# One gate of a GRU recurrence multiplied in exact bfloat16 parts, the other two in float32

## The chip, the cores and the metric

The kernel runs on one core of a Trainium2 chip. The metric is the device time of one execution in microseconds; three runs of the kernel before are given, with their median. A profile comes from one further execution with a hardware trace. In it PE is TensorE (matmuls), PEld the weight loads of TensorE, DVE VectorE, ACT ScalarE, POOL GpSimd and SP SyncE; "q" behind an engine stands for the queue on which it issues DMAs.

## The reference

A GRU runs over time. x has the shape (8, 256, 512), that is 8 rows of 256 time steps of 512 features, and the state has 8 x 512 values.

```
gi = x @ W_ih + b_ih            # 512 -> 3*512
gh = h @ W_hh + b_hh
r = sigmoid(i_r + h_r);  z = sigmoid(i_z + h_z)
n = tanh(i_n + r * h_n)
h = (1 - z) * n + z * h         # one step; 256 of them, each on the one before
```

The 2048 states then pass through a mixture of experts: a router chooses 2 of 8 experts (each 512 to 2x256 and back) by softmax and top 2, and a shared expert (512 to 2x1024 and back) takes all of them. The sum is added to x. Everything is float32.

## The kernel before

The step, which is `step(n)`. The state is kept transposed, `hT` with 128 partitions by 4 quarters `q` by 8 batch rows, in four buffers that take turns (`states`). For each gate in the order r, n, z (the order of `banks`), 16 matmuls are issued: for each quarter q of the 512 inputs, four of them (j), each with the 8 columns of hT as the stationary operand and 128 columns of w_hh as the moving one, and each writing one strip of 32 partitions of the gate's PSUM bank, rows 32j to 32j+8. In the trace each of these float32 matmuls appears as two records. Behind each gate DVE turns the bank with a 32x32 block transpose (`turned`, L489): the gate then lies with the features over the partitions. ACT takes the sigmoid of r (L493), DVE multiplies n's part by r (L496) and adds the part of x (L498), ACT takes the tanh (L500), DVE turns z, ACT takes its sigmoid (L502), and three DVE operations form the new state: `hn = h - n` (L505), `z*hn` (L507), `n + z*hn` (L508). ACT copies the new state into `hc` for the later stages (L511).

The part of x and the biases are put into a gate's bank before its matmuls accumulate onto it: `open_gate` (L458, on ACT) copies them there from `seeds` (r and z) or `seeds_n` (n). In the n bank the rows 32j to 32j+8 hold the bias of the state's product and the rows 32j+8 to 32j+16 the part of x, since r must multiply the first and not the second. `load_seeds` loads the seeds of four steps at a time from DRAM on SP's queue.

x's part is computed ahead, in blocks of 16 steps. `project(k, g)` multiplies the turned x of block k with W_ih for gate g in four pieces, and its end copies the result to `gi` on ACT (L416), adds the bias on POOL (L417) and stores it to DRAM on SP. `transpose_x(k)` (L313, on DVE) turns the block's x and issues the loads of the next one; `turn_x_afterwards` puts it into a list of things to do on DVE "afterwards".

The order of the work is written by a planner in the kernel, without times from the chip. A `queue` holds pieces of matmul work (projections, then the shared expert of finished blocks), and behind each step as many pieces are issued as keep the block even: they are the filler of TensorE while the other engines finish the step. `catch_up(room)` issues DVE work from the list `afterwards` behind each step, up to `WINDOW = 1.1` us by the planner's own costs; a piece that needs something from the list forces it. Routing (`choose`, `sum_logits`, `order_experts`, `weigh`, `count_places`, `give_places`, `send_rows`) is given fixed steps of the block. Weight loads of the experts are put into `loads` and issued one at a time on POOL's DMA queue (L170).

The tile `we` has room for the weights of 8 experts. W_ih lies in the room of experts 6 and 7 and w_hh in that of experts 4 and 5 (`wih`, `whh`) until they are no longer needed: experts 0 to 3 are loaded from block 2 on, 6 and 7 in the last block, 4 and 5 behind the loop. After the loop come the rest of the shared expert, the layout of the lists, and 35 tiles of 128 rows, each through one expert's weights (`gu_t` L722, `yp` L853).

Before the loop, block 0 is projected, x's blocks 0 and 1 are turned on TensorE, one and a half projections of block 1 are made, the list is emptied (`catch_up(None)`), the seeds of the first chunks are loaded, and the three gates of step 0 are opened. POOL's copy of one column of `hn` into `last_hn` (L506) stands in each step.

Of the kernel before, what the change touches and what calls it, by code (L numbers as in the profile page):

```python
# [9 lines left out]
F32 = mybir.dt.float32  # L10
BF16 = mybir.dt.bfloat16
I32 = mybir.dt.int32
AF = mybir.ActivationFunctionType
ALU = mybir.AluOpType
AX = mybir.AxisListType
PSUM = bass.MemoryType.PSUM

P = 128
TS = 16
SC = 4  # L20
NS = 2
NH = 4


@with_exitstack
def kernel(
# [52 lines left out]
    nc = tc.nc  # L79
    B, T, D = x.shape  # L80
    G3 = w_ih.shape[1]
    E = w_gate.shape[1]
    IM = w_down.shape[1]
    ISH = w_sh_down.shape[0]
    NQ = D // P
    NB = T // TS
# [9 lines left out]
    const = ctx.enter_context(tc.tile_pool(name="const", bufs=1))  # L96
    wts = ctx.enter_context(tc.tile_pool(name="wts", bufs=1))
    xpool = ctx.enter_context(tc.tile_pool(name="xpool", bufs=3))
    state = ctx.enter_context(tc.tile_pool(name="state", bufs=1))
    two = ctx.enter_context(tc.tile_pool(name="two", bufs=2))  # L100
# [32 lines left out]

    we = wts.tile([P, E, NW, D], F32, name="we")
    wih = we[:, E - 2 : E].rearrange("p e w n -> p (e w n)").rearrange("p (q n) -> p q n", q=NQ)
    whh = we[:, E - 4 : E - 2].rearrange("p e w n -> p (e w n)").rearrange("p (q n) -> p q n", q=NQ)
    bias = const.tile([P, G3], F32, name="bias")
    bias_h = we[:, 0, 0:2].rearrange("p w n -> p (w n)")
# [12 lines left out]
    h = state.tile([P, NQ, 32], F32, name="h")  # L151
# [41 lines left out]
    seeds = [const.tile([P, SC, 2 * P], F32, name=f"seeds_{i}") for i in range(NS)]  # L193
    seeds_n = [const.tile([P, SC, P], F32, name=f"seeds_n_{i}") for i in range(NS)]
    seed_hn = we[:, 0, 2, 0:P]
    states = [const.tile([P, NQ, 32], F32, name=f"hT_{i}") for i in range(NH)]
    nc.vector.memset(seeds[0], 0.0)
    ident = const.tile([P, P], F32, name="ident")
    make_identity(nc, ident)
# [183 lines left out]
    def catch_up(room):  # L383
        while afterwards and (room is None or afterwards[0][0] <= room):
            cost, work = afterwards.popleft()
            work()
            if room is not None:
                room -= cost
# [46 lines left out]
    def load_seeds(c, of="nz"):  # L435

        k, o = divmod(c * SC, TS)
        steps = slice(o, o + SC)
        for g in of:
            assert (k, g) in projected  # L440
            tile_, at_row, src = (
                (seeds_n[c % NS], B, gi_dram[k][0]) if g == "n" else (seeds[c % NS], 0, gi_dram[k][1])
            )
            for j in range(4):
                by = nc.sync if c else nc.scalar
                row = 32 * j + at_row
                by.dma_start(tile_[row : row + B], src[j, :, steps, :])

    def open_gate(n, g):
# [7 lines left out]
            src = seeds[c % NS][:, t].rearrange("p (a n) -> p a n", a=2)[:, "rz".index(g)]  # L457
        nc.scalar.copy(banks[g][:, 0:P], src)  # L458

    whh_v = whh.rearrange("p q (a k j i) -> p q a j k i", a=3, k=NQ, j=4)  # L460
    hc_of = {}

    def hc_of_block(k):
        return hc_of[k // 2][:, NG * (k % 2) : NG * (k % 2) + NG]

    turned_gates = {g: state.tile([P, NQ, 32], F32, name=f"{g}T") for g in "rnz"}
    hn = state.tile([P, NQ, B], F32, name="hn")
    last_hn = state.tile([P, 1], F32, name="last_hn")

    def step(n):  # L470
        k, t = divmod(n, TS)
        c, ts = divmod(n, SC)
        hT, new = states[n % NH], states[(n + 1) % NH][:, :, 0:B]
        for g, bank in banks.items():
            a = "rzn".index(g)
            for q in range(NQ):
                for j in range(4):
                    nc.tensor.matmul(  # L478
                        bank[32 * j : 32 * j + B, 0:P].rearrange("b (k i) -> b k i", k=NQ),
                        hT[:, q, 0:B],  # L480
                        whh_v[:, q, a, j, :],
                        start=False,
                        stop=(q == NQ - 1),
                        skip_group_check=True,
                    )

        def turned(g):
            gT = turned_gates[g]
            nc.vector.transpose(gT.rearrange("p a b -> p (a b)"), banks[g][:, 0:P])  # L489
            return gT  # L490

        r = turned("r")[:, :, 0:B]
        nc.scalar.activation(r, r, AF.Sigmoid)  # L493
        open_gate(n + 1, "r")
        nT = turned("n")
        nc.vector.tensor_tensor(r, nT[:, :, 0:B], r, ALU.mult)  # L496
        open_gate(n + 1, "n")
        nc.vector.tensor_tensor(r, nT[:, :, B : 2 * B], r, ALU.add)  # L498
        nn = r
        nc.scalar.activation(nn, nn, AF.Tanh)  # L500
        z = turned("z")[:, :, 0:B]
        nc.scalar.activation(z, z, AF.Sigmoid)  # L502
        open_gate(n + 1, "z")

        nc.vector.tensor_tensor(hn, hT[:, :, 0:B], nn, ALU.subtract)  # L505
        nc.gpsimd.tensor_copy(last_hn, hn[:, 0, 0:1])  # L506
        nc.vector.tensor_tensor(z, z, hn, ALU.mult)  # L507
        nc.vector.tensor_tensor(new, nn, z, ALU.add)  # L508
        if t == 0 and k % 2 == 0:
            hc_of[k // 2] = two.tile([P, 2 * NG, NQ, 32], F32, tag="hc", name=f"hc_{k // 2}")  # L510
        nc.scalar.copy(  # L511
            hc_of_block(k).rearrange("p g q (c t) -> p q g c t", t=TS)[:, :, :, :, t],
            new.rearrange("p q (g c) -> p q g c", c=2),
        )
# [390 lines left out]
        under_way.update(up=stages, turn=last)  # L905


    nc.vector.transpose(states[0].rearrange("p q b -> p (q b)"), h.rearrange("p q i -> p (q i)"))
    nc.vector.tensor_tensor(bias[:, 0 : 2 * D], bias[:, 0 : 2 * D], bias_h, ALU.add)

    first = [project(0, g) for g in range(3)]
# [9 lines left out]
    for k in range(1, NB):  # L921
        for g in range(3):
            projections.extend(project(k, g))
            if g == 1 and k + 1 < NB:
                projections.append(
                    Piece(lambda _: None, lambda k=k: turn_x_afterwards(k + 1), parts=0)
                )
# [5 lines left out]
    for _ in range(NQ + NQ // 2):  # L933
        projections.popleft().run(None)
    catch_up(None)
    load_seeds(1)
    for g in banks:
        open_gate(0, g)
    for k in range(NB):


        at = {}

        def when(t, cost, busy, work):
            at.setdefault(t, []).append((cost, busy, work))

        if k > 0:
            steps_ = (
                (choose, 1, 0), (sum_logits, 0.5, 0), (order_experts, 0, 1.2), (weigh, 0, 1.0),
                (count_places, 0.5, 0), (give_places, 0, 1.2), (send_rows, 0, 0.75),  # L950
            )
            for t, (f, cost, busy) in enumerate(steps_):
                when(t, cost, busy, lambda f=f, k=k: f(k - 1))
            if k == 1:
                when(4, 0, 0.7, lambda k=k: weigh_all(k - 1))
            for i in range(2 if k > 1 else E):
                when(6 + i if k > 1 else 5 + 4 * i // 3, 0, 0, lambda k=k, i=i: enter(k - 1, i))
        if k > 1 and k % 2:
            for b in (3, 2):
                when(6, 0, 0, lambda k=k, b=b: load_again(k - b))  # L960
        if k == 2:
            for e in range(E - 4):
                load_expert(e)
        if k == NB - 1:
            for e in (E - 2, E - 1):
                load_expert(e)
        quota = 33 * NQ if k < 2 else sum(p.left() for p in projections) / max(1, NB - 1 - k)
        while projections and quota > 0:
            quota -= projections[0].left()
            queue.append(projections.popleft())  # L970
        assert k == NB - 1 or len(projections) <= 13 * (NB - 2 - k), "the next block's are made"
        if k > 1:
            half = NSH * NF // 2
            for u in range(half):
                feed_shared(k // 2 - 1, half * (k % 2) + u)
        all_of_it = sum(p.left() for p in queue)
        all_of_it += sum(cost for pieces in at.values() for cost, _, _ in pieces)
        spent = 0.0
        for t in range(TS):
            n = k * TS + t  # L980
            step(n)
            if (n + 1) % SC == 0 and n + 1 < T and (n + 1) // SC + NS - 1 < T // SC:
                load_seeds((n + 1) // SC + NS - 1)
            room = WINDOW
            for cost, busy, work in at.get(t, ()):
                work()
                spent += cost
                room -= busy
            catch_up(room)
            if loads and (k < 2 or k == NB - 1 or t % 2):  # L990
                loads.popleft()()

            due = all_of_it * (t + 1) / TS
            while queue and (queue[0].left() == 0 or due - spent >= 0.5 * queue[0].cost):
                spent += queue[0].run(due - spent)
                if queue[0].left() == 0:
                    queue.popleft()
        assert not queue
# [2 lines left out]
    spare.extend(banks.values())  # L1001
    k = NB - 1
    assert not loads
    for e in (E - 4, E - 3):
        load_expert(e)

    MM = NQ
# [70 lines left out]
```

## Time and profile before

| | |
|---|---|
| three runs | 1448.86, 1452.12, 1456.24 us; median 1452.12 |
| the profiled execution | 1449.96 us, its span 1448.1 us |
| the first r gate starts, the last one | 36.06 us, 1176.17 us |
| records of TensorE | 33084 matmuls, 33084 weight loads |
| share of the span busy | PE 97%, PEld 74%, DVE 47%, ACT 34%, POOL 20% |
| mean granted TensorE clock | 0.991 of full speed |
| mean DMA traffic | 64 GB/s, 91.97 MB in all |

How to read it: the three gates of the loop have 8192 records each, that is 256 steps x 16 matmuls x 2. Matmul records overlap each other, so the time that a group takes is read from where the next group starts and not from the sum of its records. A line of a timeline has the start in us, the duration of the merged group in us, the engine, the line in the kernel, the operation, its tiles, and how many instructions were merged; in brackets stands the engine's idle time before it and what ended it. A line of groups has the busy time in us and the mean duration of one instruction in ns, then idle time before it.

### The profile page before, as it was taken

What the parts mean: (1) busy time and instruction counts of PE and PEld (TensorE: products, weight loads), DVE (VectorE), ACT (ScalarE), POOL (GpSimd) and SP (SyncE); (2) the same over time, 40 slices, a digit from 0 to 9 for tenths busy, and PEclk for the clock granted to TensorE, in tenths of its full rate; (3) what the DMA queues carried; (4) which work ended last, traced back from release to release, by engine and by line L of the source; (5) the groups of instructions that cost most, each with busy time, mean ns of one, the idle gap of its engine ahead of it and who ended that gap; (6) DMA issues with size and microseconds to landing.
All of it is one profiled execution on the core that took longest, in us unless ns stands there. A gap on an engine that the chain in (4) does not pass through costs nothing.

```text
span 1448.1 us, 75006 instructions
## 1 busy us (share of the span) xinstructions
PE 1398.4 (97%) x33084; PEld 1064.6 (74%) x33084; DVE 683.3 (47%) x2661; ACT 496.2 (34%) x2072; POOL 284.9 (20%) x525
## 2 busy tenths in 40 slices
PE   5999999999999999999999999999999999999995
PEld 2677778886788888889887878888887864444442
DVE  2445445544555555555545554555455552222221
ACT  0433333433333434343433333334343420222221
POOL 1333321111111101010101010101010222344442
PEclk9999999999999999999999999999999999999998
DMA  7334422122212021111011111111111424444453
GB/s 262 96 118 101 72 73 61 56 65 65 58 54 48 15 51 30 36 45 37 29 40 29 40 45 35 32 34 27 32 45 37 98 62 117 90 93 88 89 91 46
DMA packets 66949, 91.97 MB, mean 64 GB/s; under 512 B 12688, under 2 KB 44480, under 8 KB 66624
## 3 DMA queue, kind: packets, MB, share of 16 engines
q0 software_dynamic: 15104, 37.57, 12.4%
q1 hardware_dynamic: 50176, 48.60, 12.3%
q8 instruction: 261, 4.28, 1.3%
q10 hardware_dynamic: 1344, 1.00, 0.2%
q14 instruction: 64, 0.52, 0.1%
HBM read 56.80 MB, written 30.32 MB: 60 GB/s over the span
## 4 chain that ended last, share of the span: by engine, by line
PE 94%; DMA 2%; DVE 1%; issue 1%; POOL 0%; ACT 0%; DVEq 0%; SPq 0%; POOLq 0%; ACTq 0%
PE ps_r L478 16%; PE ps_n L478 16%; PE ps_z L478 15%; PE gu_s L768 15%; PE gip L324 10%; PE gu_t L722 8%; PE po L324 7%; PE yp L853 4%; DMA gid_rz<-gi 1%; DMA x<-in_x_dram 0%; DMA we<-in_L_cond_b_hh_dram 0%; PE ps_z L833 0%; PE ps_r L833 0%; PE ps_n L833 0%; DMA out_dram<-y,row 0%
## 5 line engine op out<-in xcount | busy, mean ns | idle before, releaser
L478 PE MATMUL ps_r<-we,hT 128*8 128x128 f32 x8192 | 291.8, 273 | 11.4 <-ACT ps_r L458 8.9
L478 PEld LDWEIGHTS ps_r<-we,hT 128*8 128x8 f32 x8192 | 242.8, 90 | 79.2 <-ACT ps_z L458 25.3
L478 PE MATMUL ps_n<-we,hT 128*8 128x128 f32 x8192 | 293.0, 273 | 5.0 <-issue 5.0
L478 PE MATMUL ps_z<-we,hT 128*8 128x128 f32 x8192 | 292.3, 273 | 3.0 <-issue 3.0
L768 PE MATMUL gu_s<-hc,wsu 128*32 128x256 f32 x4096 | 260.5, 379 | 1.2 <-issue 1.1
L478 PEld LDWEIGHTS ps_n<-we,hT 128*8 128x8 f32 x8192 | 240.3, 90 | 8.4 <-issue 6.6
L478 PEld LDWEIGHTS ps_z<-we,hT 128*8 128x8 f32 x8192 | 240.1, 90 | 5.8 <-issue 4.2
L506 POOL COPY last_hn<-hn 128x1 f32<-128x1 f32 x256 | 47.3, 185 | 905.0 <-DVE hn L505 902.7
L489 DVE STREAM_TRANSPOSE rT<-ps_r 128x128 f32<-128x128 f32 x256 | 81.2, 317 | 304.4 <-PE ps_r L478 304.3
L324 PE MATMUL gip<-we,xT 128*32 128x512 f32 (+3 forms) x2080 | 195.8, 489 | 7.2 <-DVE xT L313 5.4
L768 PEld LDWEIGHTS gu_s<-hc,wsu 128*32 128x32 f32 x4096 | 161.0, 110 | 52.0 <-issue 7.8
L493 ACT ACTIVATE rT<-rT 128x32 f32<-128x32 f32 x256 | 58.6, 229 | 374.8 <-DVE rT L489 374.8
L489 DVE STREAM_TRANSPOSE nT<-ps_n 128x128 f32<-128x128 f32 x256 | 81.3, 317 | 149.4 <-PE ps_n L478 149.4
L324 PE MATMUL po<-wsd,act_s 128*32 128x512 f32 (+3 forms) x1304 | 135.7, 501 | 0.7 <-DVE again L806 0.7
L722 PE MATMUL gu_t<-we,xrT 128*128 x280 | 131.6, 593 | 0.3 <-issue 0.3
L324 PEld LDWEIGHTS gip<-we,xT 128*32 128x32 f32 x2080 | 76.4, 111 | 69.3 <-issue 56.4
L458 ACT COPY ps_n<-seeds_n 128x128 f32<-128x128 f32 x256 | 69.0, 269 | 110.8 <-DVE nT L489 107.7
L511 ACT COPY hc<-hT 128x32 f32<-128x32 f32 x256 | 63.2, 247 | 88.1 <-DVE hT L508 87.4
L489 DVE STREAM_TRANSPOSE zT<-ps_z 128x128 f32<-128x128 f32 x256 | 81.2, 317 | 13.0 <-PE ps_z L478 3.9
L500 ACT ACTIVATE rT<-rT 128x32 f32<-128x32 f32 x256 | 58.7, 229 | 68.3 <-DVE rT L498 68.2
L324 PEld LDWEIGHTS po<-wsd,act_s 128*32 128x32 f32 x1304 | 52.2, 110 | 38.2 <-issue 27.4
L859 POOL DMA_INDIRECT out_dram<-y,row x35 | 55.5, 1586 | 112.8 <-DVE y L856 108.9
(164 smaller groups left out, 1193.9 us busy)
## 6 DMA issues: line engine op xcount, KB each, us to landing
we<-in_L_ffn_w_gate_up_dram POOLq DMA_DIRECT2D x32, 256.0 KB, 3.9
seeds<-gid_rz SPq DMA_DIRECT2D x252, 32.0 KB
gid_rz<-gi SPq DMA_DIRECT2D x15, 512.0 KB
wsu<-_L_ffn_w_sh_gate_up_dram POOLq DMA_DIRECT2D x16, 256.0 KB, 3.3
rows<-hr SPq DMA_DIRECT2D x128, 32.0 KB
we<-in_L_ffn_w_down_dram POOLq DMA_DIRECT2D x16, 256.0 KB, 4.5
again<-in_x_dram SPq DMA_DIRECT2D x16, 256.0 KB
out_dram<-again SPq DMA_DIRECT2D x16, 256.0 KB
```

What stands on the lines that cost most here:

```text
L324: nc.tensor.matmul(ps[32 * c : 32 * c + 32], lhs(c), rhs, start=start, stop=stop, skip_group_check=True,)
L458: nc.scalar.copy(banks[g][:, 0:P], src)
L478: nc.tensor.matmul(bank[32 * j : 32 * j + B, 0:P].rearrange("b (k i) -> b k i", k=NQ), hT[:, q, 0:B], whh_v[:, q, a, j, :], start=False, s ...
L489: nc.vector.transpose(gT.rearrange("p a b -> p (a b)"), banks[g][:, 0:P])
L493: nc.scalar.activation(r, r, AF.Sigmoid)
L500: nc.scalar.activation(nn, nn, AF.Tanh)
L506: nc.gpsimd.tensor_copy(last_hn, hn[:, 0, 0:1])
L511: nc.scalar.copy(hc_of_block(k).rearrange("p g q (c t) -> p q g c t", t=TS)[:, :, :, :, t], new.rearrange("p q (g c) -> p q g c", c=2),)
L722: nc.tensor.matmul(box["ps"], lhs(q), w_up(q), start=(q == 0), stop=(q == NQ - 1))
L768: nc.tensor.matmul(box["ps"][32 * g : 32 * g + 32, two_i, :], wsu[c][:, q, two_i, fs], hc_of[m][:, :, q, :], start=(two_i == 0 and q == 0) ...
L853: nc.tensor.matmul(box["y"], lhs, rhs, start=(f == 0), stop=(f == NF - 1))
L859: nc.gpsimd.indirect_dma_start(out=out.rearrange("b t d -> (b t) d"), out_offset=bass.IndirectOffsetOnAxis(ap=laid["row"][:, i : i + 1], a ...
```

## The change

The n part of w_hh is taken apart into three bfloat16 numbers for each float32 (`take_apart`): the high half of the float32's bits, the high half of the remainder, and the rest. They lie in `whn`, in the room of expert 3. The new state is taken apart in the same way in each step (`take_apart_state`, two DVE subtractions): `states` now has four slots of 8 columns a quarter, with the state itself in slot 2 (`NEW`), its remainders in slots 1 and 0, and zeros in slot 3. Read as bfloat16 with a stride, the high halves of the four slots are one stationary operand of 32 columns. Gate n is then 4 quarters x 3 parts of the weights x 4 strips = 48 bfloat16 matmuls; its bank holds three groups of 8 rows, one for each part of the state, and the part of x in the fourth. Behind its turn a DVE reduction sums the three groups (`gn`), before the multiplication by r. Gates r and z read slot 2 in float32 as before.

Around it: the small POOL copy reads the last part of the new state (`last_part`) instead of `hn`; the initial state is taken apart; w_hh is taken apart before the first step, on ACT and DVE; the turn of the next block's x is put into the list after projection g = 0 of the block before it instead of g = 1; expert 3 is loaded behind the loop with experts 4 and 5.

```diff
+NP = 3
+NEW = 2
...
+    whn = (
+        we[:, E - 5]
+        .rearrange("p w n -> p (w n)")
+        .bitcast(BF16)
+        .rearrange("p (q s n) -> p q s n", q=NQ, s=NP)
+    )
...
-    states = [const.tile([P, NQ, 32], F32, name=f"hT_{i}") for i in range(NH)]
+    states = [const.tile([P, NQ, 4, B], F32, name=f"hT_{i}") for i in range(NH)]
...
-                (seeds_n[c % NS], B, gi_dram[k][0]) if g == "n" else (seeds[c % NS], 0, gi_dram[k][1])
+                (seeds_n[c % NS], NP * B, gi_dram[k][0]) if g == "n" else (seeds[c % NS], 0, gi_dram[k][1])
...
+    def high(t_):
+
+        return t_.bitcast(BF16).rearrange("p (n two) -> p n two", two=2)[:, :, 1]
+
+    def take_apart(q):
+
+        w = whh[:, q, 2 * D :]
+        nc.scalar.copy(whn[:, q, 0], high(w))
+        nc.vector.tensor_tensor(w, w, high(w), ALU.subtract)
+        nc.scalar.copy(whn[:, q, 1], high(w))
+        nc.vector.tensor_tensor(whn[:, q, 2], w, high(w), ALU.subtract)
+
+    def high_of(st):
+        return st.bitcast(BF16).rearrange("p q s (b two) -> p q s b two", two=2)[..., 1]
+
+    def take_apart_state(st):
+
+        for s_ in range(NEW, 0, -1):
+            nc.vector.tensor_tensor(
+                st[:, :, s_ - 1], st[:, :, s_], high_of(st)[:, :, s_], ALU.subtract
+            )
...
-        hT, new = states[n % NH], states[(n + 1) % NH][:, :, 0:B]
+        st, st_new = states[n % NH], states[(n + 1) % NH]
+        h, new = st[:, :, NEW], st_new[:, :, NEW]
+        parts = [high_of(st)[:, q].rearrange("p s b -> p (s b)") for q in range(NQ)]
         for g, bank in banks.items():
             a = "rzn".index(g)
-            for q in range(NQ):
+            if g == "n":
+                work = [(32, parts[q], whn_v[:, q, s_]) for q in range(NQ) for s_ in range(NP)]
+            else:
+                work = [(B, h[:, q], whh_v[:, q, a]) for q in range(NQ)]
+            for i, (m, lhsT, rhs) in enumerate(work):
                 for j in range(4):
                     nc.tensor.matmul(
-                        bank[32 * j : 32 * j + B, 0:P].rearrange("b (k i) -> b k i", k=NQ),
-                        hT[:, q, 0:B],
-                        whh_v[:, q, a, j, :],
+                        bank[32 * j : 32 * j + m, 0:P].rearrange("b (k i) -> b k i", k=NQ),
+                        lhsT,
+                        rhs[:, j],
...
-        nT = turned("n")
-        nc.vector.tensor_tensor(r, nT[:, :, 0:B], r, ALU.mult)
+        nT = turned("n").rearrange("p q (s b) -> p q s b", b=B)
+        nc.vector.tensor_reduce(
+            gn, nT[:, :, 0:NP].rearrange("p q s b -> p q b s"), AX.X, ALU.add
+        )
+        nc.vector.tensor_tensor(r, gn, r, ALU.mult)
         open_gate(n + 1, "n")
-        nc.vector.tensor_tensor(r, nT[:, :, B : 2 * B], r, ALU.add)
+        nc.vector.tensor_tensor(r, nT[:, :, NP], r, ALU.add)
...
-        nc.vector.tensor_tensor(hn, hT[:, :, 0:B], nn, ALU.subtract)
-        nc.gpsimd.tensor_copy(last_hn, hn[:, 0, 0:1])
+        nc.vector.tensor_tensor(hn, h, nn, ALU.subtract)
         nc.vector.tensor_tensor(z, z, hn, ALU.mult)
         nc.vector.tensor_tensor(new, nn, z, ALU.add)
+        take_apart_state(st_new)
+        nc.gpsimd.tensor_copy(last_part, st_new[:, 0, 0, 0:1])
...
-            if g == 1 and k + 1 < NB:
+            if g == 0 and k + 1 < NB:
                 projections.append(
                     Piece(lambda _: None, lambda k=k: turn_x_afterwards(k + 1), parts=0)
                 )
...
     catch_up(None)
+    for q in range(NQ):
+        take_apart(q)
     load_seeds(1)
...
-            for e in range(E - 4):
+            for e in range(E - 5):
                 load_expert(e)
...
-    for e in (E - 4, E - 3):
+    for e in (E - 5, E - 4, E - 3):
         load_expert(e)
```

More of the change, by code (lines that the diff above doesn't have):

```diff
@@ L458, in open_gate @@
         nc.scalar.copy(banks[g][:, 0:P], src)
+    def high(t_):
[13 more added lines that the diff above has]
+            )
     whh_v = whh.rearrange("p q (a k j i) -> p q a j k i", a=3, k=NQ, j=4)
+    whn_v = whn.rearrange("p q s (k j i) -> p q s j k i", k=NQ, j=4)
     hc_of = {}
@@ L466 @@
     turned_gates = {g: state.tile([P, NQ, 32], F32, name=f"{g}T") for g in "rnz"}
-    hn = state.tile([P, NQ, B], F32, name="hn")
-    last_hn = state.tile([P, 1], F32, name="last_hn")
+    hn, gn = (state.tile([P, NQ, B], F32, name=name) for name in ("hn", "gn"))
+    last_part = state.tile([P, 1], F32, name="last_part")
     def step(n):
@@ L472, in step @@
         c, ts = divmod(n, SC)
-        hT, new = states[n % NH], states[(n + 1) % NH][:, :, 0:B]
+        st, st_new = states[n % NH], states[(n + 1) % NH]
+        h, new = st[:, :, NEW], st_new[:, :, NEW]
+        parts = [high_of(st)[:, q].rearrange("p s b -> p (s b)") for q in range(NQ)]
         for g, bank in banks.items():
             a = "rzn".index(g)
-            for q in range(NQ):
+            if g == "n":
[3 more added lines that the diff above has]
+            for i, (m, lhsT, rhs) in enumerate(work):
                 for j in range(4):
                     nc.tensor.matmul(
-                        bank[32 * j : 32 * j + B, 0:P].rearrange("b (k i) -> b k i", k=NQ),
-                        hT[:, q, 0:B],
-                        whh_v[:, q, a, j, :],
+                        bank[32 * j : 32 * j + m, 0:P].rearrange("b (k i) -> b k i", k=NQ),
+                        lhsT,
+                        rhs[:, j],
                         start=False,
-                        stop=(q == NQ - 1),
+                        stop=(i == len(work) - 1),
                         skip_group_check=True,
@@ L905, in run_tile @@
         under_way.update(up=stages, turn=last)
-    nc.vector.transpose(states[0].rearrange("p q b -> p (q b)"), h.rearrange("p q i -> p (q i)"))
+    h0T = we[:, 0, 3, 0:P].rearrange("p (q b) -> p q b", q=NQ)
+    nc.vector.transpose(h0T.rearrange("p q b -> p (q b)"), h.rearrange("p q i -> p (q i)"))
+    nc.vector.tensor_copy(states[0][:, :, NEW], h0T[:, :, 0:B])
+    take_apart_state(states[0])
     nc.vector.tensor_tensor(bias[:, 0 : 2 * D], bias[:, 0 : 2 * D], bias_h, ALU.add)
```

## The prediction

> **What bounds the kernel now.** I read the engines' shares and the chain first, then groups by shape, one step's timeline, and PE's waits.
>
> ```profile
> PE 1398.4 (97%) x33084; PEld 1064.6 (74%) x33084; DVE 683.3 (47%) x2661; ACT 496.2 (34%) x2072; POOL 284.9 (20%) x525
> ...
> PE 94%; DMA 2%; DVE 1%; issue 1%; POOL 0%; ACT 0%; DVEq 0%; SPq 0%; POOLq 0%; ACTq 0%
> ```
>
> TensorE is the bound: 94% of the chain. But half of its time is the recurrence, where a second chain runs beside it. One step:
>
> ```profile
> 702.43 1.14 PE L478 MATMUL ps_r<-we,hT 128*8 128x128 f32 x32
> 703.30 1.14 PE L478 MATMUL ps_n<-we,hT 128*8 128x128 f32 x32
> 704.18 1.14 PE L478 MATMUL ps_z<-we,hT 128*8 128x128 f32 x32
> 705.05 1.99 PE L324 MATMUL gip<-we,xT 128*32 128x128 f32 x24
> 706.77 0.40 PE L478 MATMUL ps_r<-we,hT 128*8 128x128 f32 x6
> ```
>
> DVE in the same step:
>
> ```profile
> 704.49 0.32 DVE L489 STREAM_TRANSPOSE nT<-ps_n 128x128 f32<-128x128 f32 x1 [0.56 <-PE ps_n L478]
> 704.91 0.19 DVE L496 TENSOR_TENSOR rT<-nT,rT 128x32 f32<-128x32 f32 x1
> 705.14 0.19 DVE L498 TENSOR_TENSOR rT<-nT,rT 128x32 f32<-128x32 f32 x1
> 705.37 0.32 DVE L489 STREAM_TRANSPOSE zT<-ps_z 128x128 f32<-128x128 f32 x1
> ...
> 706.22 0.19 DVE L508 TENSOR_TENSOR hT<-rT,zT 128x32 f32<-128x32 f32 x1
> ```
>
> A gate takes 0.874 us (703.30 to 704.18), three take 2.62, filler takes 1.72, and the step is 4.34. The new state ends at 706.41. The least distance anywhere from there to the next r is 0.146, so r could have begun at 706.56: 0.21 of slack. From the starts of all 256 nT transposes and the ends of all hT results in the timeline: median step 4.347, median slack 0.284, and the bare chain (steps with no slack) 4.06. Only 15 steps have no slack. A cheaper gate is therefore paid out until the chain binds.
>
> Note the tie at 705.37: add L498 ends at 705.33 and the next DVE instruction follows 0.04 later, exactly when z is there. Anything added between nT and the add delays zT and the whole chain.
>
> **The n gate.** Removed: 256 x 16 float32 matmuls, which leave 8192 records. Added: 256 x 48 bfloat16 matmuls, one record each. Rows by shape give what a float32 record costs: 273 ns at 128 columns, 379 at 256, 593 at 512, so 107 ns per 128 columns beside a fixed 166. The four 32-column strips run together: 8 sets in 0.874 us, 109 ns a set, the 107 and 2.5 more. No row here has bfloat16 at 128 columns; for that the Trainium skill, TensorE: Matmul & The Clock Gate, section "Wait — 56ns, not 53.3ns?", gives 55.6 ns from start to start, half of the 107 with some 2.5. An estimate by it: 12 sets of 56 ns, 0.67 us, which saves 0.204.
>
> The only bfloat16 work in the strips has 8 columns:
>
> ```profile
> 1187.97 0.19 PE L324 MATMUL posp<-any,tri 128*32 128x8 bf16 x4
> 1187.97 0.12 PEld L324 LDWEIGHTS <-ones 128*32 128x32 bf16 x4
> 1188.00 0.19 PE L324 MATMUL posp<-count,ones 128*32 128x8 bf16 x4
> ...
> 1188.02 0.40 PE L768 MATMUL gu_s<-hc,wsu 128*32 128x256 f32 x4
> ```
>
> Four matmuls and four weight loads of 32 columns pass in about 0.03 us, some 7 ns a pair, also between float32 neighbours, so neither the weight loads nor the change of type cost more than a set of 56. Bounds of the gate: 12 x 0.029 = 0.35 us, and 48 at the float32 pace of 0.874/32 = 27.3 ns, 1.31 us. Here a rule speaks against the change: the same section states that the start-to-start distance of matmuls never drops below about 25 ns, however few their columns. By it the gate is 48 x 25 = 1.2 us, 0.33 longer than before, and the loop 83 us longer. The row shows 7 ns, so I take 0.67; but it is a burst of 8, and this gate is a run of 48, so the rule stays a rival.
>
> **The chain of a step.** Removed: 0.204 ahead of nT. Added between nT and the product: the reduction of 96 elements a partition. Reductions here follow elements read (L607 16: 170 ns, L552 64: 220, L657 128: 286), so 0.253, with 0.034 to the next dependent instruction: 0.287. Net the chain grows by 0.083 to 4.15, while PE's step falls to 4.347 - 0.204 = 4.14. So the two meet. Taking each step's larger one over the 255 steps gives -40 us (52 without the chain). Per 0.05 us more of chain about 10 us are lost; at 0.2 more instead of 0.083 only 19 are left. The reduction's bounds: 0.16 (nearest row, 8 elements) and twice 0.253 for its strided read.
>
> The two subtractions behind the new state (0.19 each, gap 0.034, some 0.07 for a second wait, on POOL) delay n alone; in the instruction order n's first weight load has a wait on DVE of its own, so r waits for the state only. They end some 0.5 after it, n starts at 0.146 + 0.874 = 1.02: cover 0.5. If r also waited, 0.5 x 256 = 128 us would be lost. Queued behind them on DVE is the catch-up work of up to 1.1 us, then rT: rT may end at 0.5 + 1.1 + 0.32 = 1.92 after the state, nT is due at 1.94. It just fits, at no cost; longer groups (`order_experts`) lose some 0.05 in 15 steps. POOL's copy moves 0.5 later, before POOL's weight DMAs; nothing in the loop waits for these.
>
> **Before the first step.** Taking w_hh apart is 8 ACT copies and 8 DVE subtractions of 128x512, and the first gates stand behind them on ACT:
>
> ```profile
> 35.74 0.28 ACT L458 COPY ps_r<-seeds 128x128 f32<-128x128 f32 x1
> ...
> 36.06 1.89 PE L478 MATMUL ps_r<-we,hT 128*8 128x128 f32 x32 [8.93 <-ACT ps_r L458]
> ```
>
> ACT comes free of its DMA issues at 35.25, with block 1's copy of gi (L416, 0.59). Per quarter: copy 0.59 (L416's, the nearest), subtraction 0.68 (L806's), copy 0.59, two handovers of 0.1: 2.06, the second subtraction being beside it. x's turn for block 2 (L313, 1.14) now stands before them on DVE, and its loads land near 36 (last issued at 33.5). Four quarters from 37.1 end at 44.8, ps_r follows at 45.1: +9 us (7 to 11), nothing covers it. On SP, x_3's eight loads (0.3 to 0.4 each) pass the seeds of chunk 1, first needed four steps later: free. The first state's copy and two subtractions fall into ACT's wait.
>
> **x's turn ahead.** PE waits:
>
> ```profile
> PE gip L324 <- DVE xT L313: 5.4, 2, 3.4
> PE ps_n L478 <- issue: 5.0, 6, 2.0
> PE ps_z L478 <- issue: 3.0, 3, 1.3
> ```
>
> In the instruction order the turn of block 9 moves from step 67 to 52, that of block 5 stays forced (steps 20/21). So the 3.4 at 349 us goes, with the half-speed projection behind it (16 records in 3.51 us): -5 us.
>
> **Instructions.** The "issue" waits, some 10 us in all with smaller ones, fall where instruction packets (261 of 16 KB, one per 4.4 us) come late behind x and weight loads. Each step has 32 more instructions in a shorter step, 19% faster use: a stall starts earlier, 0.65 us for each of ten, and a few are new: +7 (0 to 20).
>
> **Experts.** Expert 3's six loads move behind the loop. The last of twelve is issued at 1200.7 now, each takes about 0.6 on POOL and lands in 4; the first tile starts at 1228.9. 15 us of cover: 0, and if it were gone, some 5.
>
> **Sum**, against the profiled execution's 1449.96 us: -40 + 9 - 5 + 7 = -29, 1421. The three runs' median is 2.2 above that: 1423.
>
> **Rivals.**
> 1. Slower: the run of 48 matmuls doesn't hold 14 ns. At the rule's 25 ns: +83 + 9 - 5 = +87, about 1539. For it: no long bfloat16 run exists in the trace. Against: 7 ns in the burst. It decides from 29 us/2.55 us per 0.01 us of gate, 0.11 more: a gate of 0.78 us, 16.3 ns a matmul. Chance 0.15.
> 2. The chain takes the gain: reduction or handovers 0.1 dearer, or catch-up work of DVE pushed into nT. Loop -19 to -25: 1436 to 1445, and worse with stalls. For: no slack between nT and zT. Against: reductions are regular in all rows. Chance 0.13.
> 3. Instruction supply costs 20 to 35 and not 7: 1436 to 1451. For: stalls cluster in the first 5 blocks. Against: fewer weight loads there. Chance 0.07.
> The likeliest, 1406 to 1436, has 0.65.
>
> **How the numbers follow.** A difference of 0.5%, 7 us, is what a measurement can tell. The likeliest case is all faster (0.65). Of rival 2, 0.09 is faster and 0.04 within; of rival 3, 0.03 faster, 0.02 within, 0.02 slower; rival 1 is slower (0.15). Together 0.77, 0.06, 0.17. The range leaves out the bulk of rival 1 and a little below: 1404 to 1465.
>
> **What would show it.** Right: n to z 0.67 us, nT to zT 1.16 instead of 0.88, most r starts 0.146 behind the state, the first r near 45, no wait of gip near 349, 219 ns a bfloat16 record. Wrong: n to z at 0.87 or more (rival 1), step median above 4.2 with n at 0.67 (rival 2), PE's "issue" beyond 20 us (rival 3), or r waiting on L486's results.

## The result and the profile after

The changed kernel takes 1498.45 us (median of 4 runs, 1491.26 to 1505.13), the kernel before 1450.49 beside it (1447.03 to 1456.24). The ratio is 1.0326 with a 95% interval of 1.0263 to 1.0389: slower, where 1423 was predicted. The profiled execution took 1501.47 us, its span 1499.7. Runs more than 1.5% above the fastest of their kernel are left out of all comparisons; there is one, of e9.

From the page of the changed kernel: the engines' busy times with their instructions, the queue that brings instructions (packets, MB, share), the chain by engine, and the new gate's group (busy us, mean ns, idle before).

```profile
PE 1380.9 (92%) x37172; PEld 1009.8 (67%) x37172; DVE 841.3 (56%) x3440; ACT 497.8 (33%) x2080; POOL 285.1 (19%) x525
...
q8 instruction: 293, 4.80, 1.3%
...
PE 85%; DVE 6%; issue 5%; DMA 2%; ACT 1%; POOL 0%; DVEq 0%; SPq 0%; POOLq 0%; ACTq 0%
...
L515 PE MATMUL ps_n<-we,hT 128*32 128x128 bf16 x12288 | 248.1, 220 | 6.0 <-issue 5.6
```

PE is busy for less time than before and yet the run is longer: its share of the chain fell from 94% to 85%, and "issue" rose from 1% to 5%. That word stands for an engine that waits for nothing the profile shows. DVE's share rose too, from 1% to 6%; it is 8% in e2 below, which is faster than both kernels, so this share is not the loss. The clock is not it either: the mean granted clock is 0.988, against 0.991 before and 0.987 in e2. One step in PE's timeline:

```profile
699.78 1.06 PE L515 MATMUL ps_r<-we,hT 128*8 128x128 f32 x32
700.66 0.86 PE L515 MATMUL ps_n<-we,hT 128*32 128x128 bf16 x48
701.33 1.06 PE L515 MATMUL ps_z<-we,hT 128*8 128x128 f32 x32
702.20 0.62 PE L809 MATMUL gu_s<-hc,wsu 128*32 128x256 f32 x6
703.46 1.67 PE L809 MATMUL gu_s<-hc,wsu 128*32 128x256 f32 x25 [0.64 <-issue]
704.78 0.40 PE L515 MATMUL ps_r<-we,hT 128*8 128x128 f32 x6
```

Gate n takes 701.33 - 700.66 = 0.67 us, what the prediction had. The step is 5.00 us long all the same, since PE stood still in its filler for 0.64 with nothing to wait for. DVE in that step:

```profile
701.56 0.32 DVE L526 STREAM_TRANSPOSE nT<-ps_n 128x128 f32<-128x128 f32 x1 [0.34 <-PE ps_n L515]
701.91 0.27 DVE L533 TENSOR_REDUCE gn<-nT 128x32 f32<-128x96 f32 x1
702.28 0.19 DVE L536 TENSOR_TENSOR rT<-gn,rT 128x32 f32<-128x32 f32 x1
...
703.51 0.19 DVE L547 TENSOR_TENSOR hT<-rT,zT 128x32 f32<-128x32 f32 x1
703.74 0.49 DVE L486 TENSOR_TENSOR hT<-hT 128x32 f32<-128x32 f32 x2
```

The state ends at 703.70, 3.92 behind the start of r (3.98 before). PE's waits (us in total, times, longest) say where the time is lost:

```profile
PE ps_z L515 <- issue: 38.7, 43, 2.1
PE ps_r L515 <- ACT ps_r L466: 17.6, 1, 17.6
PE gu_s L809 <- issue: 9.0, 16, 1.5
PE ps_r L515 <- DVE hT L547: 7.3, 16, 0.8
PE ps_n L515 <- issue: 5.6, 9, 2.9
...
PE gip L332 <- DVE xT L321: 3.8, 1, 3.8
```

Before, the largest "issue" waits were 5.0 and 3.0 us. Now the gate behind n alone loses 38.7. The steps, taken from the ends of all 256 hT results from the second block on: the lower quarter is 4.144 us long (before 4.336), so the undisturbed step is as forecast. But the sum of what the others are longer than this quarter rose from 41.6 to 121.0 us.

The gaps tell what they are. In the list of single instructions the first four lie before matmul records 1879, 2007, 2134 and 2262, 127 or 128 apart, and others follow at multiples of that. PE's and PEld's 74,344 records over 293 packets of 16 KB are 254 a packet, or 127 of each kind, so such a gap stands where one packet's instructions end. Not every packet has one: the loop has 280 packets. Of the 90 gaps over 0.25 us between the first r and the last state, 73, worth 60.6 us, end 1.2 to 1.7 us after a packet of q8 has landed, though these windows cover only 12% of that time (280 x 0.5 us of 1188). This reads as PE having run out of instructions; the experiments test it.

### The profile page after: what moved, and what is told of

It reads as the page before. It is cut to its first block, busy times and chain, and to the rows that moved or that the text cites. A ratio compares the mean times of both kernels' runs of the same rounds, so it can differ in the third digit from the quotient of the medians.

```text
span 1499.7 us, 84064 instructions
## 1 busy us (share of the span) xinstructions
PE 1380.9 (92%) x37172; PEld 1009.8 (67%) x37172; DVE 841.3 (56%) x3440; ACT 497.8 (33%) x2080; POOL 285.1 (19%) x525
## 4 chain that ended last, share of the span: by engine, by line
PE 85%; DVE 6%; issue 5%; DMA 2%; ACT 1%; POOL 0%; DVEq 0%; SPq 0%; POOLq 0%; ACTq 0%
PE ps_r L515 15%; PE gu_s L809 15%; PE ps_z L515 14%; PE ps_n L515 11%; PE gip L332 8%; PE gu_t L763 8%; PE po L332 7%; PE yp L894 4%; DVE eq L590 1%; DMA gid_rz<-gi 1%; DVE nT L526 1%; DVE gn L533 1%; DVE rT L538 0%; ACT rT L540 0%; DMA x<-in_x_dram 0%
## 5 line engine op out<-in xcount | busy, mean ns | idle before, releaser
L515 PE MATMUL ps_z<-we,hT 128*8 128x128 f32 x8192 | 301.4, 273 | 38.9 <-issue 38.7
L515 PE MATMUL ps_r<-we,hT 128*8 128x128 f32 x8192 | 301.3, 274 | 28.9 <-ACT ps_r L466 17.6
L809 PE MATMUL gu_s<-hc,wsu 128*32 128x256 f32 x4096 | 267.7, 380 | 9.0 <-issue 9.0
L515 PEld LDWEIGHTS ps_z<-we,hT 128*8 128x8 f32 x8192 | 221.8, 90 | 53.5 <-issue 51.7
L515 PE MATMUL ps_n<-we,hT 128*32 128x128 bf16 x12288 | 248.1, 220 | 6.0 <-issue 5.6
L549 POOL COPY last_part<-hT 128x1 f32<-128x1 f32 x256 | 47.1, 184 | 984.4 <-DVE hT L486 929.4
L515 PEld LDWEIGHTS <-hT 128*32 128x32 bf16 x12288 | 225.5, 97 | 8.6 <-issue 7.8
L332 PEld LDWEIGHTS gip<-we,xT 128*32 128x32 f32 x2064 | 81.2, 111 | 71.5 <-issue 57.9
L486 DVE TENSOR_TENSOR hT<-hT 128x32 f32<-128x32 f32 x514 | 98.9, 192 | 36.5 <-DVE hT L486 1.8
L754 DVE TENSOR_TENSOR act_t<-gu_t,act_t 128x256 f32<-128x256 f32 x35 | 14.9, 425 | 131.4 <-ACT act_t L750 131.4
```

Of the source, the lines that this page charges most:

```text
L332: nc.tensor.matmul(ps[32 * c : 32 * c + 32], lhs(c), rhs, start=start, stop=stop, skip_group_check=True,)
L486: nc.vector.tensor_tensor(st[:, :, s_ - 1], st[:, :, s_], high_of(st)[:, :, s_], ALU.subtract)
L515: nc.tensor.matmul(bank[32 * j : 32 * j + m, 0:P].rearrange("b (k i) -> b k i", k=NQ), lhsT, rhs[:, j], start=False, stop=(i == len(work) ...
L549: nc.gpsimd.tensor_copy(last_part, st_new[:, 0, 0, 0:1])
L809: nc.tensor.matmul(box["ps"][32 * g : 32 * g + 32, two_i, :], wsu[c][:, q, two_i, fs], hc_of[m][:, :, q, :], start=(two_i == 0 and q == 0) ...
```

## Experiments

Theory S: instructions arrive too late once r, n and z take 64 + 96 + 64 = 224 of them (matmuls and weight loads by their records) in 2.42 us instead of 192 in 2.62. Theory B: bfloat16, or the change of type, disturbs PE. Theory D: the added VectorE work makes the steps longer.

**e2_n_wide: the same columns in a third of the instructions.**

```diff
-                work = [(32, parts[q], whn_v[:, q, s_]) for q in range(NQ) for s_ in range(NP)]
+                work = [(32, parts[q], whn_w[:, q]) for q in range(NQ)]
...
-                        bank[32 * j : 32 * j + m, 0:P].rearrange("b (k i) -> b k i", k=NQ),
+                    out = bank[32 * j : 32 * j + m, 0 : NP * P if g == "n" else P]
```

> The changed kernel with the three parts of a weight slice streamed by one matmul of 384 columns into three blocks of the bank, so 16 weight loads and 16 matmuls for gate n instead of 48 and 48, for the same columns; only the first block is turned and used, so two of the three parts of w_hh are left out of n. Theory S: 160 instructions a step for r, n and z, no more gaps than before, PE's step of 4.14 holds in nearly all steps, time 1405 to 1430. Theory B: the same bfloat16 columns stand at the same place, so the gaps stay, 1480 to 1500. Theory D: VectorE's work is unchanged, so 1480 to 1500 too.

Measured: 1407.75 us against 1451.77, ratio 0.9699 (0.9669 to 0.9728). Two steps of its timeline, then its waits:

```profile
704.03 1.06 PE L517 MATMUL ps_r<-we,hT 128*8 128x128 f32 x32
704.90 0.84 PE L517 MATMUL ps_n<-we,hT 128*32 128x384 bf16 x16
705.55 1.06 PE L517 MATMUL ps_z<-we,hT 128*8 128x128 f32 x32
706.43 1.92 PE L811 MATMUL gu_s<-hc,wsu 128*32 128x256 f32 x32
708.24 0.95 PE L517 MATMUL ps_r<-we,hT 128*8 128x128 f32 x28
```

```profile
PE ps_r L517 <- DVE hT L549: 11.0, 25, 1.0
...
PE ps_z L517 <- issue: 2.1, 3, 0.9
...
PE ps_n L517 <- issue: 1.1, 2, 0.9
```

Gate n takes 0.65 us, the same 6144 columns in bfloat16 as the changed kernel's 0.67, with the same VectorE work, and the "issue" waits of n and z fall from 44.3 to 3.2 us. (Two of its three blocks of columns are never read, so it measures time and does not replace the kernel.) The loop (first r to last state) is 1094.9 us, against 1187.9 in the changed kernel and 1144.4 before. Its chain by engine:

```profile
PE 86%; DVE 8%; issue 2%; DMA 2%; ACT 1%; POOL 0%; DVEq 0%; ACTq 0%; SPq 0%; POOLq 0%
```

B and D fall as explanations of these 93 us; S stands.

**e4_small_pairs: only the instructions, in the kernel before.**

```diff
+            if g == "n":
+                for i in range(NQ * 4):
+                    j = i % 4
+                    nc.tensor.matmul(bank[32 * j : 32 * j + 32, P : P + 8], tri[:, 0:32], ones[:, 0:8],
+                        start=False, stop=True, skip_group_check=True)
```

> The kernel before the change, with 16 bfloat16 matmuls of 8 columns (and their 16 weight loads) put behind gate n of each step, into columns that nothing reads: 32 more instructions a step (224 in all for r, n and z), next to no columns. Their own time is 16 pairs of 7 to 14 ns, 0.11 to 0.22 us a step, 28 to 57 us over the loop if all of it is on PE's path. Theory S: gaps like those of the changed kernel come on top (40 to 80 us): 1500 to 1570, and waits called issue at ps_z of some 40 us. Theory B: a change of type costs what it costs in the changed kernel, without waits called issue at packet boundaries: 1480 to 1530. Theory D: own time alone, 1478 to 1507, at most 25 gaps.

Measured: 1521.77 us, ratio 1.0496 (1.046 to 1.0531). In its timeline and waits:

```profile
1223.80 0.27 PE L489 MATMUL ps_n<-ones,tri 128*32 128x8 bf16 x15
...
1223.92 0.60 PE L478 MATMUL ps_z<-we,hT 128*8 128x128 f32 x14
1226.76 0.71 PE L478 MATMUL ps_z<-we,hT 128*8 128x128 f32 x17 [2.24 <-issue]
```

```profile
PE ps_z L478 <- issue: 23.2, 30, 2.2
```

The 16 pairs pass in 0.10 us (1223.80 to 1223.90), 26 us over 256 steps; the time rose by 70. The other 44 came with 30 waits of z for instructions, where the kernel before has 3. These are 23.2 us, where some 40 were expected, and all waits for instructions over 0.25 us in the loop are 30.5 us against 10.0 before. That is about half of the 44; the other half is not idle time of PE, and these waits do not show what it is. Of its 46 gaps over 0.25 us, 40 end 1.2 to 1.7 us after a packet. S's mark, without any of the changed arithmetic.

**e7_pairs_spread: the same pairs elsewhere.** They stand in the filler, behind its first three quarters of a slice.

```diff
             while queue and (queue[0].left() == 0 or due - spent >= 0.5 * queue[0].cost):
-                spent += queue[0].run(due - spent)
+                ran = queue[0].run(min(due - spent, 3) if first else due - spent)
+                spent += ran
+                if first and ran:
+                    small_pairs()
+                    first = False
```

> The kernel with the 16 small pairs of e4_small_pairs (columns that nothing reads), but put into the other work between z and the next r, behind its first three quarters of a slice, instead of behind gate n. The same number of instructions a step and the same own time. If it is the dense run of instructions that outruns their supply (theory S, burst: 224 in a row within 2.5 us): few waits called issue, 1470 to 1490, own time alone. If it is the number of instructions per step (theory S, amount): gaps and time as in e4_small_pairs, 1510 to 1530.

Measured: 1482.63 us against 1455.69 beside it, ratio 1.0201 (1.0172 to 1.0229): 27 us, about the pairs' own time.

```profile
PE ps_n L491 <- issue: 5.5, 4, 2.3
PE ps_r L491 <- issue: 4.3, 8, 1.5
...
PE ps_z L491 <- issue: 2.7, 3, 1.2
```

No fewer instructions (37,660 matmul records against 37,180 in e4), but the dense run of r, n and z is 192 again. It is the burst that outruns the supply, not the number per step. The average leaves room: in the changed kernel's loop packets start every 4.07 us (median), and the shortest intervals are 3.3.

**e3_two_parts and e10_two_parts_again: a shorter burst.** One edit: `range(NP - 1)` for the parts of the weights.

> The changed kernel without the products of the third part of w_hh: 32 weight loads and 32 matmuls for gate n instead of 48 and 48, gate n about 0.45 us instead of 0.67, PE's step of work about 3.92 and below the bare chain of 4.07. Theory S: 192 instructions as before the change, in 2.2 us: fewer gaps than the 92 of the changed kernel though more than the 19 of before, time 1390 to 1430. Theory B: a third of the bfloat16 work goes, so a third of the loss at the most: 1455 to 1485. Theory D: unchanged VectorE work, 1480 to 1500.

> e3_two_parts once more, beside the other two of this call. In its first run steps 6 and 7 of a block took 4.2 us. If the stall at these steps belongs to the session and not to the kernel: they take what they take in the other kernels of this call (5.0 in all, 1400 us; or 4.2 in all, 1384 us). If it belongs to the kernel: 4.2 here and 1380 to 1388 whatever the others do.

Measured: 1384.49 and 1383.14 us, ratios 0.9531 (0.9483 to 0.958) and 0.9531 (0.9494 to 0.9569). The burst has 192 instructions in 2.19 us, 11.4 ns each and nearly as dense as the changed kernel's 10.8, yet n and z wait for instructions for 5.1 and 9.1 us only (e3's waits, then e10's):

```profile
PE ps_z L515 <- issue: 3.0, 3, 1.3
PE ps_n L515 <- issue: 2.1, 2, 1.8
```

```profile
PE ps_n L515 <- issue: 6.2, 3, 3.5
...
PE ps_z L515 <- issue: 2.9, 2, 2.7
```

So the length of the burst matters and not only its density. Both leave out the third part's products; e3 ended 5.5 us below its expected range.

**e1, e5, e11: gate n in float32 again**, with all else of the change kept (in e5 and e11 with w_hh as it is):

```diff
-            if g == "n":
-                work = [(32, parts[q], whn_v[:, q, s_]) for q in range(NQ) for s_ in range(NP)]
-            else:
-                work = [(B, h[:, q], whh_v[:, q, a]) for q in range(NQ)]
+            work = [(B, h[:, q], whh_v[:, q, a]) for q in range(NQ)]
```

> The changed kernel with gate n's products in float32 again (16 float32 matmuls on what the parts leave of w_hh in place, so its n isn't the reference's); the stacked state, the reduction, the two subtractions, the setup and x's earlier turn stay. Theory S (TensorE's instructions arrive too late once r, n and z take 224 of them in 2.42 us instead of 192 in 2.62): 192 again, gaps of PE over 0.25 us as before (about 19, not 92), median step 4.35, time 1450 to 1465 (the setup's 9 us stay, x's turn gives 0 to 5). Theory B (bfloat16 itself, or changing between the types, disturbs PE): the same 1450 to 1465. Theory D (the added VectorE work makes the steps longer): the steps stay near 4.39 and the time stays at 1480 to 1500.

> The changed kernel with gate n's products in float32 from w_hh as it is; the parts are still made at the start (their remainder goes to other columns), and the stacked state, the reduction, the two subtractions and x's earlier turn stay. In the first kernel of this kind n was another one, and the part behind the loop took 302 us instead of 267, since other experts were chosen. Theory S (instructions too late): no such waits, the loop near 1151 us as in that kernel, the start 8 us longer than before, 267 us behind the loop: 1460 to 1470. Theory D (VectorE's additions make the loss): 1490 to 1500.

> e5_n_float32_whole once more. It took 1481 us where 1460 to 1470 was expected; its steps 6 and 7 took 5.05 us against 4.56 in e1_n_float32, whose TensorE program is the same, and these two steps of 15 blocks make 15 us. If that stall belongs to the session: 1464 to 1468 here when e10 shows none, 1481 when e10 shows it too. If to the kernel: 1481 either way.

Measured: e1 1499.57 us, which looked like D; but its loop was 1151.7 us and 34 of its excess lay behind the loop (301.9 us against 267.4), where other experts had been chosen. e5 1481.29, ratio 1.0175 (1.0152 to 1.0197); e11 1462.82, ratio 1.0078 (1.0051 to 1.0105). e5's miss by 11 us sits in the two steps of each block that follow the issue of its indirect DMAs (called 6 and 7 above): 5.05 us each against 4.56. In the timeline of e5, at the first of them, the weight loads stop as GpSimd's indirect DMA ends:

```profile
885.00 0.99 POOL L658 DMA_INDIRECT listed<-said,pl  x1 [0.48 <-issue]
...
885.83 1.44 PE L512 MATMUL ps_z<-we,hT 128*8 128x128 f32 x30
...
886.30 0.68 PEld L512 LDWEIGHTS ps_z<-we,hT 128*8 128x8 f32 x26 [0.37 <-issue]
```

Gate z takes 1.44 instead of 1.06. The same kernel in a later session and on another chip (e11) takes 4.55 to 4.57 at these steps in most blocks, so the stall does not belong to the kernel alone. It does not belong to the session alone either: e6 (below) and e7, run in e5's session and on its chip, take 4.56 to 4.63 and 4.66 to 4.79 us there. The two kernels of that session with the stall, e5 and e8, are made from the changed kernel, the two without it from the one before. What it is stays open. By the medians of e11 the rest of the change costs 12 us, by the profiles 14.5 (the first r is 6.6 later, the loop 8.3 longer, the part behind it 0.4 shorter). In the loop, one place shows the VectorE work, behind `order_experts` (DVE's timeline of e11):

```profile
855.06 0.49 DVE L486 TENSOR_TENSOR hT<-hT 128x32 f32<-128x32 f32 x2
855.47 0.22 DVE L585 TENSOR_TENSOR gt<-lg 128x64 f32<-128x64 f32 x1
855.61 0.22 DVE L586 TENSOR_TENSOR eq<-lg 128x64 f32<-128x64 f32 x1
855.86 1.34 DVE L587 TENSOR_TENSOR eq<-eq,before 128x64 f32<-128x64 f32 x1
...
857.63 0.31 DVE L523 STREAM_TRANSPOSE rT<-ps_r 128x128 f32<-128x128 f32 x1
```

With the two subtractions ahead, the group keeps rT until 857.63, 2.6 us behind the state's end at 855.03. That step takes 4.94 us; steps 3 to 5 together lose 7.0 us over 11 blocks (3 and 5 to 14).

**e6_turn_only: x's turn alone**, `g == 1` to `g == 0` in the kernel before.

> The kernel before with x's turn queued behind gate r's projection instead of behind z's, and nothing else. The prediction's sum has 5 us for it, from a wait of 3.4 us for xT near 349 us and its neighbour at half the clock: 1445 to 1448 against 1451. If the freed time only lets another wait come, no difference within 3 us. If the turn now stands in front of the step's own VectorE work, 1453 to 1460.

Measured: 1445.87 us against 1455.69, ratio 0.994 (0.9918 to 0.9961): faster by 6 to 12. Its wait:

```profile
PE gip L324 <- DVE xT L313: 3.2, 1, 3.2
```

Against the trace of before (the state's ends taken as the blocks' bounds), block 4 loses its wait and its half-clock projection (-7.0 us), block 1 waits longer for its turn (+3.5), block 2 is 2.7 shorter, and the others differ by 1.1 at most. The whole loop is 3.5 us shorter by these two profiles.

**e8_two_halves and e9_halves_enter_later: a version to beat both.** Two float16 parts of w_hh and of the state instead of three bfloat16 ones:

```diff
+        nc.scalar.activation(whn[:, q, 0], w, AF.Copy, scale=WS)
+        nc.vector.scalar_tensor_tensor(whn[:, q, 1], w, WS, whn[:, q, 0], ALU.mult, ALU.subtract)
...
+        nc.vector.tensor_scalar(half[:, :, 0], st, HS, None, ALU.mult)
+        nc.vector.scalar_tensor_tensor(half[:, :, 1], st, HS, half[:, :, 0], ALU.mult, ALU.subtract)
...
+        nc.vector.tensor_tensor(gn, nT[:, :, 0], nT[:, :, 1], ALU.add)
+        nc.vector.scalar_tensor_tensor(r, gn, 1.0 / (WS * HS), r, ALU.mult, ALU.mult)
```

The bias in the n bank is scaled by 64 x 1024 too. e9 adds one edit: `when(9 + i ...)` instead of `when(6 + i ...)` for `enter` from block 2 on.

> A version meant to beat both kernels: gate n from two float16 parts of w_hh (scaled by 64) and two of the state (scaled by 1024), all four products, so 32 weight loads and 32 matmuls as in e3_two_parts but with 22 bits of each factor; the two rows are added by one VectorE addition in place of the reduction, the scale goes into the multiplication that follows, and the setup takes one ScalarE and one VectorE pass a slice instead of two of each. Theory S: as in e3_two_parts (192 instructions for r, n and z) or a little better, since the chain is some 0.15 us shorter and PE's step of about 3.92 sets the pace: 1360 to 1385. Theory B (the two-byte type disturbs PE): no better than e3_two_parts, 1384 or more. Theory D: it has the least VectorE work of these, 1375 to 1400.

> e8_two_halves with the two indirect DMAs of each block (what GpSimd writes into the list of rows) issued behind steps 9 and 10 instead of 6 and 7. In e8_two_halves steps 6 and 7 of each block took 5.0 us where those around them took 3.9, and TensorE stood still while GpSimd made such a transfer. If the indirect DMA stalls TensorE: steps 9 and 10 take 5.0 and 6 and 7 take 4.2, time 1390 to 1396 as before. If it is something else at steps 6 and 7 (the rows' store on SyncE's queue): they stay at 5.0. If it is the placement of that session: they come down in this kernel and in e10 and e11 alike, 1370 to 1380.

Measured: e8 1394.18 us, ratio 0.9589 (0.9564 to 0.9613), with the stall at the steps called 6 and 7 (5.0 us here too); e9 1368.64 (three runs), ratio 0.9436 (0.9382 to 0.949), in a session where e10 and e11 show none. So e9 doesn't tell what the later indirect DMA is worth. Both versions beat both kernels. Of the expected range, 1360 to 1385, e8 missed the upper end by 9 us, which the extra 0.75 us (against e3's 4.26) in each of the two steps of 14 blocks covers. In e8 the first r starts at 38.23 us, 2.2 us later than before the change, where the changed kernel's starts 8.3 later.

## Why the prediction was wrong, by its own steps

**Instructions, +7 (0 to 20): the step that failed.** It took the ten or so stalls of before, let each start 0.65 us earlier and added a few. The changed kernel's loop is 92.9 us longer than that of e2, where the same columns and the same VectorE work need 160 instructions instead of 224 (some 5 of this are e2's shorter gate). Where +7 was put, the term is thus some 80 to 90. Rival 3 named the mechanism and its mark, "issue" beyond 20 us, but sized it 20 to 35 and gave it 0.07. What was held against it, fewer weight loads in the first blocks, doesn't bear: each 100 us of the loop has gaps, and packets take as long as before (1.02 us in the median of both). The error was to scale the stalls there were. They grow out of proportion: with 192 instructions in 2.62 us (before) or 2.19 (e3, e10) the loop waits 7.5 to 11.5 us for instructions (18 in e8 and e9), with 224 in 2.42 (the changed kernel) 61.3, with 224 in 2.72 (e4) 30.5, and e4 shows 44 us in all for 32 more of the smallest kind. Where between 192 and 224 the loss sets in, and how sharply, no run tells.

The sum with what the profiles measured, against 1449.96: loop without the supply's loss -49.4 (e2's), supply +92.9, start +8.3, is 1501.8; the profiled execution took 1501.47. That it closes proves nothing, as the supply's term is the difference of two of these loops; that the term is the supply's rests on e2, e4 and e7.

**The n gate, 0.67 us: right**, and with it rival 1 is out. 48 matmuls of 128 columns hold 0.67/48 = 14 ns from start to start over the whole run, in four strips. The floor of about 25 ns that the Trainium skill states (TensorE: Matmul & The Clock Gate, section "Wait — 56ns, not 53.3ns?") was weighed against the change and would have made it 1.2 us; the row that spoke for 7 ns in a burst was the better guide, and the mean record is 220 ns (219 foreseen).

**The chain, 4.15 us: too long, at no cost.** Steps without slack measure 4.07 in the changed kernel. The reduction takes 0.27 (0.253 foreseen), but nT to zT is 1.06 in the median (0.87 before) where 1.16 was foreseen, and e11 puts the whole lengthening at 4.287 - 4.06 = 0.227 and not 0.287. The loop's -40 agrees with e2: of its -49.4, some 5 are its shorter gate and 3.5 to 5 x's turn, which leaves about -40. In part that is luck, since two errors offset each other: the chain was taken 0.06 too long, and `order_experts`, next, cost 7 us that were put near nothing.

**The two subtractions, free: right for r, wrong for one group.** r waits for the state (L547), never for L486. For `order_experts` 0.05 us in each of 15 steps was foreseen; it was 0.64 in each of 11 blocks.

**Before the first step, +9: right.** First r at 44.41 instead of 36.06, 8.3 us; 45.1 was forecast. **x's turn, -5: the right size.** The loops of e6 and before differ by -3.5 in their profiles, the medians by 6 to 12. No wait of gip is left near 349 us, but one of 3.8 us came at 144: the wait was in part moved, not removed.

## What to carry to other kernels

Count the instructions of the densest stretch of an engine and not only its columns: a split into narrower types that triples the matmuls can use up its gain, and more, in fetching them. Where "issue" is in PE's waits already, compare the length of that stretch, in instructions and in time, with the time from a packet's start to its first use. As a limit this is a suggestion that no run here tried; instructions in a sparse stretch were free of it here, and so were fewer, wider matmuls.

## What was not expected of the hardware

A packet of 16 KB brings some 254 instructions, takes 0.9 to 1.4 us (the middle eighty of a hundred), and PE goes on 1.2 to 1.7 us after it has landed. From a packet's start to its use these make 2.1 to 3.1 us, as long as the burst of r, n and z, so a packet that is asked for near the beginning of a burst would come too late. This is argued: when a packet is asked for, no run measured.

Behind such a gap the four strips fall out of step: at 705.65 to 705.95 records of r and n alternate. Gaps over 0.25 us make only 54 of the 93 us (74.6 in the changed kernel's loop, 20.2 in e2's). Much of the rest lies in the same steps: counted from r to r, the 73 steps in which a wait for instructions begins are together 81 us above the lower quarter, of which the waits are 61; e2 has 6 such steps, 6 us. That this surplus is the disorder of the strips is argued from this stretch, not shown.

The reuse of weights was not tried: the 48 matmuls use only 16 different stationary operands, but each bfloat16 matmul is built with a weight load of its own, 12288 in the trace. With 16 loads, n would have 64 instructions, as in float32.
